# Turning the normalised x: VectorE's 32x32 blocks and DMAs in place of TensorE's transpose

## The chip, the core and the metric

One core of one Trainium2 chip. The core has TensorE (PE; its weight loads are listed as PEld), VectorE (DVE), ScalarE (ACT), GpSimd (POOL) and SyncE (SP), and 16 DMA engines. The metric is the device time of one execution in microseconds, lower is better; the time before is the median of 3 runs. A profile is one execution taken by the hardware profiler; its span runs from the first to the last instruction.

## What is computed

A cross-attention block followed by a feed-forward block, in float32, over 16 batches of 64 tokens with 512 features (1,024 tokens, handled as 8 tiles of 128).

```python
def layernorm(x): return (x - mean(x)) / sqrt(var(x) + 1e-5)

# attention: 32 heads of 128
q = layernorm(x) @ Wq;  k = ctx @ Wk;  v = ctx @ Wv          # 512 -> 4096 each
score = q k^T / sqrt(128) + position_bias;  masked softmax
x = x + (probs @ v) @ Wo                                     # 4096 -> 512
# feed-forward: a base layer and 8 low-rank experts with router weights
y = layernorm(x)
x = x + y @ base_W^T + base_b + experts(y)
```

The product `layernorm(x) @ Wq` needs the normalised x with its features on the partitions, so each tile [128 tokens, 512 features] must be turned. That turn is what the change touches.

## The kernel before, in words

**Matmuls.** Every large product is a float32 product split into a high and a low part (`split`, lines 69 to 71: ScalarE casts the high part, VectorE subtracts to get the low part), and each step is three TensorE matmuls (`mm3`, line 256). The K, V and Q projections also use a seven-product Strassen-Winograd scheme (`winograd`, line 213): seven steps in the order 1, 2, 6, 5, 7, 4, 3, with sums on VectorE or ScalarE after each (`post`): c11 after step 2, c22 after 7, c21 after 4, c12 after 3. c22 and c12 read the same PSUM bank `yb`: step 3 adds to it after c22 has been read.

**Stages.** First K and V for all heads, written to DRAM (`kd`, `vd`). The stages are listed in line 377: "k" stages (`keys_of`, 7 x 12 matmuls, weights `in_wk`) and "o" stages (values, 7 x 24 matmuls, weights `in_wv`). Each stage's weights are loaded two stages ahead, or as soon as buffers are free, and turned into sums (line 161 for wk, line 193 for wv) and hi/lo parts (`gh`, `gl`) one stage ahead. Results go out through 8 blocks of pool "ob" (kd stores at line 336, vd stores at 341). In the four key stages q = 3, 4, 5, 6 two tiles of x each are loaded (`x_tile`, line 321), normalised (`norm`, lines 87 to 100: statistics on VectorE, a power on GpSimd, the scaling on ScalarE) and turned (`x_turn`, line 325, called after steps 5 and 3). The stages q = 4 and q = 5 follow each other directly; q = 3 and q = 6 stand between value stages. The four 128x512 buffers of pool "v" hold x and its normalised copy, and later the loaded v.

**After it.** The turned x (`xT`) is read by GpSimd for eight differences (`tt`, line 132) and by ScalarE and VectorE for hi/lo parts, all for the query products, which begin beside the last key stage. Then, head pair by head pair, scores, softmax, the products with v and the output projection; in that part the probabilities are already turned by VectorE in 32x32 blocks, with four DMAs a head (`turned_p`, lines 490 to 502: `pb`, then `pt<-pb`). Last the feed-forward block.

**What sets the order.** TensorE's order is the program's (`manual_schedule`). In the K and V part the order on VectorE, ScalarE, GpSimd and on SyncE's queue, which issues all DMAs but one, is set when the program is built, by a scheduler with its own estimate of times; on the chip each engine and the queue run it strictly in that order. A DMA whose data isn't ready holds all that stand behind it in SyncE's queue. DMAs signal through eight completion semaphores used in turn.

Of the kernel before, what the change touches and what calls it, by code (L numbers as in the profile page):

```python
# [9 lines left out]
F32 = mybir.dt.float32  # L10
# [9 lines left out]
P = 128  # L20
D = 512
KC = D // P
# [25 lines left out]
def xattn_ffn_kernel(ctx: ExitStack, tc: tile.TileContext, x, ctxT, wq, wk, wv, wo, fside, mask,  # L48
                     base_wT, base_b, arT, router_b, lora_b, expert_map, out):
    nc = tc.nc  # L50
# [15 lines left out]
    def blk(tag, name, dt=F32, shape=(P, 512)):  # L66
        return pools[tag].tile(list(shape), dt, tag=tag, name=name)
# [34 lines left out]
    def transposed(ps, xn):  # L102
        for kc in range(KC):
            nc.tensor.transpose(ps[:, kc * P:(kc + 1) * P], xn[:, kc * P:(kc + 1) * P], ident)  # L104
# [4 lines left out]
    with ExitStack() as actx:  # L109
# [6 lines left out]
        def small_bank(name):  # L116
            return pss.tile([P, 512], F32, tag="s", name=name)
# [205 lines left out]
            return xn, xt  # L323

        def x_turn(t, xn):
            ps = small_bank("pst")
            transposed(ps, xn)
            a, g = divmod(t, 4)
            dst = xT.rearrange("p k (g a b) -> p g a k b", g=4, a=2)[:, g, a]
            nc.scalar.copy(dst, ps.rearrange("p (k b) -> p k b", k=KC))  # L330

        stored, copied = [], []

# [12 lines left out]
        with tc.manual_schedule(engines={nc.tensor.engine}):  # L346
# [15 lines left out]
            def keys_of(q, g):  # L362
                xn = {}
                for i in winograd(mm_weights(tc_, g), 2, emit_k(q)):
                    if 3 <= q < 7:
                        t = 2 * (q - 3)
                        if i in (1, 6):
                            xn[i] = x_tile(t + (i == 6))
                        if i in (6, 7):
                            with tc.issue_after(copied[-1].ins):  # L370
                                norm(sm, *([a] for a in xn[1 if i == 6 else 6]))
                        elif i == 5:
                            x_turn(t, xn[1][0])
                        elif i == 3:
                            x_turn(t + 1, xn[6][0])
# [61 lines left out]
            def load_v(p):  # L437
                v = []
                for w in range(4):
                    v.append(blk("v", "v", F32, (P, 2, 256)))  # L440
                    nc.sync.dma_start(out=v[w], in_=vd[p // 2][:, p % 2, 2 * w:2 * w + 2, :])
                return v
# [148 lines left out]
            v = load_v(0)  # L591
# [11 lines left out]
            for p in range(NP):  # L603
# [3 lines left out]
                for c in steps:  # L607
                    if c == "P":
# [3 lines left out]
                        v = load_v(p)  # L612
# [269 lines left out]
```

## Time and profile before

| | |
|---|---|
| median of 3 runs | 768.36 us (767.52 to 769.46) |
| the profiled execution: its time, its span | 768.93 us, 767.1 us |
| TensorE busy (share of the span) | 756.0 us (99%), granted clock 1.00 throughout |
| VectorE, ScalarE, GpSimd busy | 559.8 (73%), 416.8 (54%), 124.7 us (16%) |
| DMA | 80,849 packets, 124.68 MB, mean 163 GB/s |
| `pst<-ident,xn` on TensorE | 32 transposes of 128x128, 272 ns each, from 113 to 258 us |
| `xT<-pst` on ScalarE | 8 copies of 128x512, 586 ns each |
| `xn<-xt` on ScalarE | 8 of 128x512, 818 ns each |
| VectorE in 20 us stretches from 110 to 270 | 11.5 to 14.9 us busy |

How to read it: lines such as L336 are lines of the kernel. A group is line, engine, operation, out<-in and count; `ps<-wh,oh` means that tile ps is written from tiles wh and oh, with buffer numbers left out. SPq is SyncE's queue: its durations are those of issuing a DMA, while "to landing" is from the issue until the data has arrived. Matmuls overlap one another, so the durations of single matmuls add up to more than the time they take together. The chain of waits is followed back from the last instruction to whatever released each step.

### The profile page before, as it was taken

The numbers are of one execution on the slowest core, as the hardware profiler recorded it, in microseconds if no ns is written. First come the engines' busy times: TensorE is split into PE (matmuls) and PEld (weight loads), VectorE is DVE, ScalarE is ACT, GpSimd is POOL, SyncE is SP. The second block draws the span as 40 slices with busy tenths as digits, with TensorE's granted clock in tenths as the row PEclk, the third lists the DMA queues.
The fourth block names the chain that finished last, engine by engine and source line by source line (L and its number), as shares of the span: only waits on it lengthen the run. The fifth ranks groups of instructions, "written<-read, shape, count | busy, mean of one in ns | idle before, by whom it ended". The sixth has DMA issues, their size and how long they took to land.

```text
span 767.1 us, 16662 instructions
## 1 busy us (share of the span) xinstructions
PE 756.0 (99%) x6186; PEld 627.9 (82%) x6186; DVE 559.8 (73%) x1068; ACT 416.8 (54%) x1165; POOL 124.7 (16%) x143
## 2 busy tenths in 40 slices
PE   8999999999999999989999999999999999999998
PEld 6888888888888888867888888888887888888898
DVE  7986666566655765878778777787768777878975
ACT  6654455445554545667654665556545664475361
POOL 0000000000000522233220222022210222010330
PEclk9999999999999999999999999999999999999999
DMA  7785546464635446476544554446543654462011
GB/s 260 239 276 191 187 160 214 135 209 151 200 130 178 138 132 206 145 235 197 186 138 143 159 191 163 139 132 199 171 144 111 200 183 130 133 198 85 2 54 57
DMA packets 80849, 124.68 MB, mean 163 GB/s; under 512 B 9728, under 2 KB 30976, under 8 KB 80768
## 3 DMA queue, kind: packets, MB, share of 16 engines
q1 hardware_dynamic: 80624, 123.56, 49.7%
q8 instruction: 48, 0.79, 0.4%
q14 instruction: 33, 0.27, 0.1%
q10 hardware_dynamic: 144, 0.06, 0.0%
HBM read 83.74 MB, written 35.65 MB: 156 GB/s over the span
## 4 chain that ended last, share of the span: by engine, by line
PE 91%; DVE 4%; ACT 2%; issue 1%; DMA 1%; SPq 0%; POOL 0%; DVEq 0%; ACTq 0%; POOLq 0%
PE ps L259 73%; PE yz L259 5%; PE ps L728 5%; PE ps L513 4%; PE pss L466 4%; ACT p L477 1%; DMA cT<-in_ctxT 1%; PE pst L104 0%; DVE gl L71 0%; DVE bs L694 0%; DVE pb L494 0%; PE pt L104 0%; DVE p L485 0%; ACT bh L70 0%; DVE ol L71 0%
## 5 line engine op out<-in xcount | busy, mean ns | idle before, releaser
L530 DVE TENSOR_TENSOR acc<-acc,ps 128x512 f32<-128x512 f32 x128 | 87.0, 682 | 24.8 <-PE ps L259 24.0
L477 ACT ACTIVATE p<-p,nm 128x64 f32<-128x64 f32 x256 | 85.8, 338 | 34.0 <-DVE nm L471 31.7
L259 PE MATMUL ps<-wh,oh 128*128 128x512 f32 x256 | 100.1, 391 | 0.0
L259 PE MATMUL ps<-wh,ol 128*128 128x512 f32 x256 | 99.7, 390 | 0.1
L259 PE MATMUL ps<-wl,oh 128*128 128x512 f32 x256 | 99.7, 389 | 0.0
L70 ACT CAST gh<-s 128x512 fp32r<-128x512 f32 (+1 forms) x128 | 64.2, 514 | 62.7 <-PE ps L259 50.5
L71 DVE TENSOR_TENSOR gl<-s,gh 128x512 fp32r<-128x512 f32 (+1 forms) x128 | 70.5, 555 | 33.0 <-ACT gh L70 32.9
L161 POOL TENSOR_TENSOR s<-rq 128x256 f32<-128x256 f32 x32 | 25.2, 787 | 250.1 <-DMA rq<-in_wq 193.0
L71 DVE TENSOR_TENSOR ol<-ps,oh 128x512 fp32r<-128x512 f32 x64 | 39.8, 683 | 33.7 <-ACT oh L70 33.6
L71 DVE TENSOR_TENSOR gl<-raw,gh 128x512 fp32r<-128x512 f32 x48 | 34.6, 722 | 35.0 <-ACT gh L70 24.5
L70 ACT CAST gh<-raw 128x512 fp32r<-128x512 f32 x48 | 29.8, 622 | 53.9 <-PE yz L259 36.6
L259 PEld LDWEIGHTS ps<-wh,ol 128*128 128x128 f32 x256 | 48.1, 188 | 10.3 <-DVE ol L71 0.5
L259 PEld LDWEIGHTS ps<-wl,oh 128*128 128x128 f32 x256 | 48.1, 188 | 10.0
L259 PEld LDWEIGHTS ps<-wh,oh 128*128 128x128 f32 x256 | 48.0, 188 | 10.0
L477 ACT ACTIVATION_READ_ACCUMULATOR p<-p,nm 128x1 f32 x256 | 48.4, 189 | 0.0
L561 DVE TENSOR_TENSOR q<-u,ps 128x512 f32<-128x512 f32 x48 | 32.8, 684 | 21.2 <-PE ps L259 15.5
L457 POOL TENSOR_TENSOR bm<-bm,maskb 128x512 f32<-128x512 f32 x32 | 41.7, 1324 | 37.8 <-DMA bm<-in_fside 37.8
L96 POOL TENSOR_TENSOR rs<-rs,nhalf 128x1 f32<-128x1 f32 x8 | 4.4, 549 | 243.8 <-DVE rs L95 243.8
L70 ACT CAST gh<-rq 128x256 fp32r<-128x256 f32 x48 | 19.3, 404 | 37.3 <-PE ps L259 33.4
L70 ACT CAST oh<-ps 128x512 fp32r<-128x512 f32 x64 | 33.1, 589 | 11.3 <-PE ps L513 11.3
L513 PEld LDWEIGHTS ps<-pt,v 64*64 64x64 f32 x2048 | 32.1, 135 | 6.4 <-issue 6.4
L550 ACT COPY u<-ps 128x512 f32<-128x512 f32 x48 | 27.8, 579 | 17.1 <-PE ps L259 7.2
(259 smaller groups left out, 1989.3 us busy)
## 6 DMA issues: line engine op xcount, KB each, us to landing
kd<-c SPq DMA_DIRECT2D x64, 256.0 KB, 2.2
vd<-c SPq DMA_DIRECT2D x64, 256.0 KB, 2.6
kT<-kd SPq DMA_DIRECT2D x64, 256.0 KB, 4.1
v<-vd SPq DMA_DIRECT2D x64, 256.0 KB, 4.0
raw<-in_wk SPq DMA_DIRECT2D x32, 256.0 KB, 3.9
raw<-in_wv SPq DMA_DIRECT2D x32, 256.0 KB, 4.1
rq<-in_wq SPq DMA_DIRECT2D x32, 256.0 KB, 3.9
bm<-in_fside SPq DMA_DIRECT2D x32, 256.0 KB, 4.4
```

Source lines behind the costliest of these rows:

```text
L70: first = nc.scalar.copy(hi, src)
L71: return first, (lo_eng or nc.vector).tensor_tensor(lo, src, hi.bitcast(F32), ALU.subtract)
L161: self.eng.tensor_tensor(r, a, b, op)
L259: nc.tensor.matmul(o, lhsT=a, rhs=b, start=first and n == 0, stop=last and n == 2, skip_group_check=True)
L457: nc.gpsimd.tensor_tensor(bm, bm, maskb, ALU.add)
L466: nc.tensor.matmul(ps[a * S:(a + 1) * S, t, :], lhsT=qT[n // 8][:, cq], rhs=kT[m // 8][:, ck], start=True, stop=True)
L477: nc.scalar.activation(p[:, t, :], p[:, t, :], AF.Exp, bias=nm[:, t:t + 1], accum_out=sme[:, t:t + 1])
L513: nc.tensor.matmul(ps[a][d:d + S, t * S:(t + 1) * S], lhsT=v[t // 2][r, t % 2, c], rhs=pt[r, :, t, :], start=True, stop=True)
L530: return nc.vector.tensor_tensor(acc[:, t, :], acc[:, t, :], ps, ALU.add)
L550: copy = nc.scalar.copy(s[i], b["x"])
L561: add = nc.vector.tensor_tensor(self.blocks[key], s[u], b[bk], ALU.add)
L728: nc.tensor.matmul(o, lhsT=a, rhs=b, start=start, stop=stop, skip_group_check=True)
```

## The change

Only `x_turn` differs. Before, four TensorE transposes with the identity wrote a PSUM bank, and ScalarE copied the bank to its place in `xT`. Now VectorE transposes the tile in 32x32 blocks from `xn` into a new block `xb` (pool "v", the same four buffers), and 16 DMAs on SyncE's queue, one for each pair of block row i and block column j, carry 32 partitions x 4 runs of 32 floats to their place in `xT`.

```diff
         def x_turn(t, xn):
-            ps = small_bank("pst")
-            transposed(ps, xn)
+
             a, g = divmod(t, 4)
             dst = xT.rearrange("p k (g a b) -> p g a k b", g=4, a=2)[:, g, a]
-            nc.scalar.copy(dst, ps.rearrange("p (k b) -> p k b", k=KC))
+            xb = blk("v", "xb", F32, (P, 4, KC, 32))
+            nc.vector.transpose(xb, xn.rearrange("p (k j i) -> p j k i", k=KC, j=4))
+            for j in range(4):
+                for i in range(4):
+                    nc.sync.dma_start(out=dst[32 * j:32 * j + 32, :, 32 * i:32 * i + 32],
+                                      in_=xb[32 * i:32 * i + 32, j])
```

In the built program the scheduler's order around it moves too. On SyncE's queue the 16 DMAs of tiles 0, 1, 2, 3, 6 and 7 stand ahead of the stores of the steps that follow; those of tiles 4 and 5 stand together, 32 in a row, ahead of five wv loads (`raw<-in_wv`) that were issued earlier before. The loads of the later x tiles stand behind the DMAs of earlier ones. On VectorE the statistics of tile 2 stand ahead of a c22 sum, and a sum of two wv loads (line 193) stands between the first and the second c22 sum of the value stage that follows q = 5.

## The prediction

> **What bounds the kernel now.** I read the page's chain first, then the same chain in order of time around the change (90 to 320 us), then single lines and tiles, then the timelines of VectorE and of SyncE's queue. The chain:
>
> ```profile
> PE 91%; DVE 4%; ACT 2%; issue 1%; DMA 1%; SPq 0%; POOL 0%; DVEq 0%; ACTq 0%; POOLq 0%
> ```
>
> TensorE sets the end. In the stretch that the change touches it never pauses (20.00 us busy in every 20 us from 90 to 330), and its own transposes are links of the chain (start, length, what):
>
> ```profile
> 89.93 23.57 PE ps L259 x104
> 113.50 0.44 PE pst L104 x4
> 113.94 8.22 PE ps L259 x36
> 122.16 0.44 PE pst L104 x4
> ```
>
> So all that leaves TensorE here shortens the time, as long as nobody else then comes late. The question is who does; the change hands 128 DMAs to SyncE's queue, which issues in a fixed order, so I read what an issue costs there and on VectorE (min/median/max ns), and how long a landing takes:
>
> ```profile
> L336 SPq DMA_DIRECT2D kd<-c x64: 319/320/694, 17.6 to 324.2; - x64
> L341 SPq DMA_DIRECT2D vd<-c x64: 512/514/690, 56.8 to 297.6; - x64
> L501 SPq DMA_DIRECT2D pt<-pb x128: 507/584/1564, 338.0 to 705.2; - x128
> 344.32 2.41 SPq L501 DMA_DIRECT2D pt<-pb  x4
> L644 SPq DMA_DIRECT2D sar<-in_arT x2: 384/402/420, 668.8 to 669.2; - x2
> L494 DVE STREAM_TRANSPOSE pb<-p x32: 698/703/712, 336.6 to 701.9; 128x512 f32<-128x512 f32 x32
> raw<-in_wv SPq DMA_DIRECT2D x32, 256.0 KB, 4.1
> pt<-pb SPq DMA_DIRECT2D x128, 32.0 KB, 1.9
> ```
>
> pt<-pb is the nearest relative of the new DMAs: SBUF to SBUF, 32 partitions. Its issue is dearer (0.58) than a 128-row store to HBM (0.32). Four in a row took 2.41 us, 0.60 each with the gaps.
>
> **Removed from TensorE.** Eight groups of four 128x128 transposes. The chain gives a group 0.44 us; the period gives a little more: from the first transposes (113.34) to the next (122.00) are 8.66 us with 36 matmuls of 0.2267 between, which leaves 0.50. 8 x 0.50 = 4.0 us, all on the path. A rule speaks against the change here: the Trainium skill, "VectorE: DVE Perf Modes", The three transpose paths, gives TensorE 390 ns for one 128x128 bf16 transpose and VectorE 311 ns for blocks only, and advises TensorE for a full 128x128. By that figure 32 transposes would free 12.5 us; the trace's row, pipelined, frees 4.0. I take the row: the prize is 0.5%.
>
> ScalarE loses eight copies xT<-pst of 0.586 us; it was under 60% busy here, so that gives nothing. The bank of pss that a turn took isn't waited for either before or after.
>
> **Added on VectorE.** Eight block transposes of 0.70 us, 5.6 us in the 145 us from 113 to 258. In each 20 us there VectorE is busy 11.5 to 14.9; 0 to 1 us on the path, I take 0. If the cover were gone, it would be at most 5.6.
>
> **Added on SyncE: the step that decides.** Sixteen DMAs a tile. Their data is nothing: the trace's packet records have 11 ns for a 128-byte packet (five of them) beside 46 for 1 KB and 84 for 2 KB; 2,048 packets on 16 engines are an estimated 1.4 us a tile. The issue is what counts. Let d be the time from one of these issues to the next. From below 0.60, the pt<-pb row. For the third dimension (32x4x32, 128 runs of 128 bytes) the trace has two neighbours: sar<-in_arT, split in runs on one side, costs no more than a plain load (0.40 beside 0.33 to 0.42), but vd<-c costs 0.19 more than kd<-c. So d is 0.60 to 0.80; I take 0.64, since sar has the same kind of shape, and vd differs in rows (256) too. Sixteen are 10.2 us (at 0.80: 12.8), against 19.1 us for a whole key stage with two tiles, where SyncE has some 7 us of its own to issue.
>
> Here the Trainium skill, "DMA: Bandwidth & Descriptors", Anatomy of one DMA and Rules for kernel authors, also speaks against the change: about 2.0 us fixed per DMA, and below 64 KB mostly overhead. If one waited for another, 64 DMAs at 2.04 would be 131 us and the kernel would end far above 840. The row says that they overlap: 0.60 apart though each lands after 1.9. The built program has eight completion semaphores in turn, so each DMA waits for the one eight before it: 1.9/8 = 0.24 us, below d. I take the row.
>
> **Who stands behind them in the queue.** In the built program's order the first tile's 16 come before six kd stores, the second's before four vd stores, six wv loads, the next x tile and two wk loads. The stores have eight blocks, and a block is next wanted a stage later, so stores 10 us late hold nobody; the wk and wv loads run a stage or more ahead. At d = 0.64 that first burst has caught up by 147; VectorE's statistics of the third x tile, ahead of a c22 sum, wait perhaps a microsecond, with more than 5 to spare.
>
> The dangerous run is tiles 2 to 5, in two key stages that follow each other, 64 DMAs in one chain. Times are those of the trace, with TensorE ahead by 0.5 per turn removed:
> - Tile 2 normalised 170.5 - 1.0, block transpose 0.7: 170.4 with a little queueing. 16 x 0.64: 180.6. Six stores at 0.38: 182.9. 16 more: 193.1. Tile 4's load and two stores, 1.3; tile 5's load lands 2.9 later: 197.3.
> - VectorE is held at that tile's statistics. From there statistics, a weight sum, small steps, two c12 sums, one gl and the block transpose: 4.7 us, so tile 4 is turned at 202.0. The c12 sums are done by 201, wanted at 203.1.
> - 32 x 0.64 without a pause: 222.5. Behind them stand five wv loads; the fourth is issued 1.4 later and lands 4.1 after: 228.0.
> - In the new VectorE order the sum s of two of those loads stands in front of the c22 sum of the second block. Before:
>
> ```profile
> 223.72 0.69 DVE L193 TENSOR_TENSOR s<-raw,raw 128x512 f32<-128x512 f32 x1
> 225.91 0.69 DVE L232 TENSOR_TENSOR c<-u,ps 128x512 f32<-128x512 f32 x1 [0.72 <-ACT u L230]
> 234.57 0.39 PE L259 MATMUL ps<-gh,t3h 128*128 128x512 f32 x1
> ```
>
> That c22 must have read its bank before TensorE's step at 234.57, which is 231.6 after six turns are gone. It would be done at 228.0 + 0.7 + 0.7 = 229.4. So 2.2 us are left, and each 0.01 of d uses 0.64 of them: the cover is gone at d = 0.675, and behind it the stall is 64 x (d - 0.675).
>
> The last two tiles repeat the first burst. They are turned near 270 instead of 259; GpSimd's eight tt subtractions (12.2 us) then end near 284, and its next sum ran at 281.8 to 282.6 for a use on ScalarE after 299. Hidden. After 330 nothing differs but the start.
>
> **Sum.** -4.0 + 0 (VectorE) + 0 (queue, d = 0.64) = -4.0 on the profiled execution, 768.93 with a span of 767.1. The median of the runs is 768.36, 0.6 lower; on it the forecast is 764.4. I leave 0.2 for small waits: 764.6.
>
> **Rivals.**
> 1. *The queue of tiles 2 to 5 holds TensorE.* With vd's extra 0.19, d = 0.80: the chain ends 64 x 0.125 = 8.0 us late, -4.0 + 8.0 = +4.0, 772.4. It ends above before from d = 0.74 on. For it: pt<-pb is already dearer than any HBM issue, and vd shows that shape can cost 0.19. Against it: sar. With d = 0.85 it is 775.6, and I let the range end there.
> 2. *Partly eaten.* d between 0.70 and 0.775: the stall is 1.6 to 6.4, the time 766 to 771, middle 768.3.
> 3. *The gain is lost behind the stage.* TensorE is earlier by 4 at 330, but the first pair of heads has waits on ScalarE (3.1 us at 346) and on transfers; if one of those is fixed in time, half comes back: 766.5. Against it: all of them hang on chains that start from TensorE.
> 4. *VectorE becomes the bound* through the 5.6 us: it has over 5 us idle in each 20, so at most 770. Unlikely.
>
> **How the numbers follow.** Forecast, d up to 0.70: 0.46, 764.3 to 766. Rival 2: 0.17. Rival 1: 0.28. Rival 3: 0.05. Rival 4 and waits that I haven't seen: 0.04. A measurement of this kernel can tell about 0.3% (2.3 us) from no change, so the bounds are 766.1 and 770.7. Faster 0.46; same takes rival 3 and nearly all of rival 2, 0.19; slower takes rival 1, what is left of rival 2, and the unseen: 0.35. The likeliest case alone is 764.0 to 766.0; the range that should hold 8 in 10 is 763.9 to 775.6.
>
> **What would show it.** Right: no pst on TensorE's chain, 8 STREAM_TRANSPOSE of 0.70, xT<-xb issues 0.60 to 0.68 apart, TensorE without a gap from 90 to 330, and the wv loads behind the long burst issued near 222 to 224. Wrong: issues at 0.75 or more apart; TensorE waiting near 232 for a c22 sum, with VectorE idle on a wv load before it; or TensorE waiting near 203 for a c12 sum with VectorE idle on an x tile. A landing of these DMAs above 5 us would put the eight semaphores in charge, which my sum excludes.

## The result, and the profile after

The changed kernel takes 770.61 us (median of 8 runs, 768.48 to 771.78) against 768.33 for the kernel before beside it: ratio 1.0028, 95% interval 1.0016 to 1.0040. The profiled execution took 770.77 us with a span of 769.0; before it was 768.93 and 767.1. The forecast was 764.6. So the direction was wrong, and the text's first rival, the queue of tiles 2 to 5 that holds TensorE, is what came; but it came at an issue spacing at which the text had excluded it.

First the page's chain, shares of the span by engine:

```profile
PE 88%; DVE 4%; DMA 3%; SPq 2%; ACT 1%; issue 1%; POOL 0%; DVEq 0%; POOLq 0%; ACTq 0%
```

TensorE has given three points to transfers and SyncE's queue. The single lines (min/median/max ns, first and last start) show that the new parts cost what was forecast, and one thing besides:

```profile
L333 SPq DMA_DIRECT2D xT<-xb x128: 585/599/1712, 114.5 to 275.6; - x128
...
L330 DVE STREAM_TRANSPOSE xb<-xn x8: 702/703/715, 113.8 to 259.5; 128x512 f32<-128x512 f32 x8
...
L340 SPq DMA_DIRECT2D kd<-c x64: 319/327/2266, 17.9 to 326.2; - x64
```

Sixteen issues take 10.27 to 10.36 us, so d is 0.645; 0.64 was forecast. But the maxima of the first and third line, 1.71 and 2.27 us for one issue, both lie in the run of tiles 2 to 5. SyncE's queue there (start, length, what):

```profile
170.73 10.36 SPq L333 DMA_DIRECT2D xT<-xb  x16
181.19 3.01 SPq L340 DMA_DIRECT2D kd<-c  x6
184.26 10.27 SPq L333 DMA_DIRECT2D xT<-xb  x16
194.57 0.59 SPq L321 DMA_DIRECT2D xt<-in_x  x1
195.27 2.74 SPq L340 DMA_DIRECT2D kd<-c  x2
198.06 0.42 SPq L321 DMA_DIRECT2D xt<-in_x  x1
...
205.42 21.72 SPq L333 DMA_DIRECT2D xT<-xb  x32
227.19 2.49 SPq L188 DMA_DIRECT2D raw<-in_wv  x5
```

It is the order of the forecast, each piece a little later than there. VectorE behind it (in brackets, its idle time before the instruction and who ended that):

```profile
199.20 0.69 DVE L92 BATCH_NORM_STATS2 bs<-xt 128x6 f32<-128x512 f32 x1 [4.17 <-DMA xt<-in_x]
...
222.05 0.69 DVE L232 TENSOR_TENSOR c<-u,ps 128x512 f32<-128x512 f32 x1 [0.86 <-ACT u L230]
233.54 0.69 DVE L193 TENSOR_TENSOR s<-raw,raw 128x512 f32<-128x512 f32 x1 [10.81 <-DMA raw<-in_wv]
234.15 0.68 DVE L232 TENSOR_TENSOR c<-u,ps 128x512 f32<-128x512 f32 x1
...
248.07 1.27 DVE L223 TENSOR_TENSOR c<-u,ps 128x512 f32<-128x512 f32 x2
...
254.33 0.70 DVE L92 BATCH_NORM_STATS2 bs<-xt 128x6 f32<-128x512 f32 x1 [2.43 <-DMA xt<-in_x]
```

VectorE stands still for 10.81 us in front of a weight sum, with the c22 sum that TensorE needs right behind it. And TensorE:

```profile
234.89 0.50 PE L259 MATMUL ps<-gh,t3h 128*128 128x512 f32 x1 [2.62 <-DVE c L232]
...
257.82 0.50 PE L259 MATMUL ps<-t3h,gh 128*128 128x512 f32 x1 [0.65 <-DVE c L232]
```

The first wait is the c22 sum just seen; the second is one stage later, where the statistics of tile 7 stand before a c22 sum and wait 2.43 us for their x load. No burst stands right ahead of that load. It was issued at 249.75 behind two key stores whose sums VectorE, still late, made only at 248.07 (242.93 and 244.34 in the kernel before, where the load left at 245.48). Neither of TensorE's two waits exists in the kernel before. The busy time in stretches of 2 us (PE, PEld, DVE, ACT, POOL, then granted clock, DMA share, GB/s) shows a third loss:

```profile
232.00:234.00 2.00, 0.27 (x2) 0.00 (x0) 0.46 (x1) 0.00 (x0) 0.00 (x0) 1.00 0.97 355
...
236.00:238.00 2.00, 2.00 (x6) 1.63 (x5) 2.00 (x5) 1.95 (x5) 0.00 (x0) 0.50 1.16 355
```

Right after the wait TensorE is at half clock: six matmuls in 2 us, 0.43 apart where 0.227 is usual. The clock record says from 235.85 for 3.413 us. Half of that time, 1.7 us, is lost.

A ledger comes from the same bank copy of ScalarE (u<-ps) in both traces, after minus before:

| time in the kernel before | 111 | 147 | 189 | 216 to 225 | 240 | 265 to 327 | end of span |
|---|---|---|---|---|---|---|---|
| us | +0.3 | -0.7 | -1.6 | -2.5 | +2.1 | +2.0 | +1.9 |

Each pair of turns gives 0.9 to 1.0, as forecast. Between 225 and 240 it loses 4.6: the wait of 2.6, the half clock 1.7, and 0.3 that I put down to the refill of TensorE behind the wait. The pair of tiles 6 and 7 should have given 0.95 more and gave 0.1, because of the second wait.

### The profile page after: what moved, and what is told of

It reads as the page before. It is cut to its first block, busy times and chain, and to the rows that moved or that the text cites. A ratio compares the mean times of both kernels' runs of the same rounds, so it can differ in the third digit from the quotient of the medians.

```text
span 769.0 us, 16702 instructions
## 1 busy us (share of the span) xinstructions
PE 755.5 (98%) x6154; PEld 626.7 (81%) x6154; DVE 561.2 (73%) x1076; ACT 411.7 (54%) x1157; POOL 124.8 (16%) x143
## 4 chain that ended last, share of the span: by engine, by line
PE 88%; DVE 4%; DMA 3%; SPq 2%; ACT 1%; issue 1%; POOL 0%; DVEq 0%; POOLq 0%; ACTq 0%
PE ps L259 70%; PE yz L259 5%; PE ps L732 5%; PE ps L517 4%; PE pss L470 4%; SPq L333 1%; DVE gl L71 1%; ACT p L481 1%; DMA cT<-in_ctxT 1%; DMA slb<-in_lora_b 1%; DMA raw<-in_wv 1%; DMA xt<-in_x 1%; DVE bs L698 0%; PE pt L104 0%; DVE s L161 0%
## 5 line engine op out<-in xcount | busy, mean ns | idle before, releaser
L71 DVE TENSOR_TENSOR gl<-s,gh 128x512 fp32r<-128x512 f32 (+1 forms) x128 | 72.1, 567 | 24.5 <-ACT gh L70 24.3
```

The costliest lines, as they stand in the source:

```text
L71: return first, (lo_eng or nc.vector).tensor_tensor(lo, src, hi.bitcast(F32), ALU.subtract)
```

## The experiments

Ten kernels, in three groups that each shared a chip with the kernel before (768.75, 769.12 and 769.26 us). The queue theory ("theory A" in four of the texts): what stands behind the issues in SyncE's queue lands late, VectorE, which works in a fixed order, waits for it, and TensorE then waits for VectorE. The rival, the order theory (B): the added work of VectorE and the rearranged order cost by themselves. The scheduler set the order anew for each of these kernels, so none of them holds the order of VectorE fixed.

**one_dma**: the sixteen become one, which leaves out the exchange of the blocks between partitions.

```diff
-            for j in range(4):
-                for i in range(4):
-                    nc.sync.dma_start(out=dst[32 * j:32 * j + 32, :, 32 * i:32 * i + 32],
-                                      in_=xb[32 * i:32 * i + 32, j])
+            nc.sync.dma_start(out=dst, in_=xb.rearrange("p j k i -> p (j k i)").rearrange("p (k b) -> p k b", k=KC))
```

> One DMA a tile in place of 16; VectorE's block transposes stay, and so does the removal of TensorE's. Leaves out the exchange of blocks between partitions. Theory A (the 16 issues a tile on SyncE's queue make the wv loads and x loads late, and TensorE then waits for c22 sums): nothing is late, 764.6 +- 0.8, no TensorE wait for a c22 sum, clock 1.00 until 340. Theory B (the added VectorE work or the reordered engines cost the time, not the queue): 769 to 771.

Measured: 764.82 us, ratio 0.9952 (0.9934 to 0.9971). VectorE's block transposes are all there, and the forecast's 764.6 is met; so the transposes cost nothing that shows. The order did change: the weight sum of 233.54 stands ahead of both c22 sums here (also in eight, five and pool_queue), as in the kernel before. That place is no kinder to a late load, so it does not explain the gain; no run here shows more of the order by itself. VectorE's waits for transfers (total us, times, longest), first in the changed kernel:

```profile
DVE bs L92 <- DMA xt<-in_x: 14.9, 6, 5.4
DVE s L193 <- DMA raw<-in_wv: 13.2, 3, 10.8
```

and with one DMA:

```profile
DVE s L193 <- DMA raw<-in_wv: 2.1, 2, 1.3
...
DVE bs L92 <- DMA xt<-in_x: 1.3, 1, 1.3
```

The lateness of x and wv loads is gone with the issues.

**eight** and **twenty** change the number of issues. eight: two DMAs for each 32 partitions, not exchanged. twenty: the four diagonal blocks are cut in two.

```diff
+            for c in range(4):
+                for h in range(2):
+                    r = slice(32 * c, 32 * c + 32)
+                    nc.sync.dma_start(out=dst[r, 2 * h:2 * h + 2, :], in_=...)
```

> Eight DMAs a tile in place of sixteen, each of twice the bytes; it leaves out the exchange of blocks between partition groups, so the same bytes go to other places. Queue theory: a tile takes 5.1 us of SyncE's queue, a pair 10.3; the chain that ended 2.6 us late with 41 us of issues for four tiles is 20 us shorter, so no load is late: 764.8 us, 763.8 to 766.5, as with one and with five. If the loss grows in proportion to the issues (0 at 1, 5.8 at 16), 767.5. Order theory: 768 to 771.

```diff
+                for i, ks in ((i, ks) for i in range(4) for ks in (((0, 2), (2, 4)) if i == j else ((0, 4),))):
+                    ks = slice(*ks)
+                    nc.sync.dma_start(out=dst[32 * j:32 * j + 32, ks, 32 * i:32 * i + 32],
+                                      in_=xb[32 * i:32 * i + 32, j, ks])
```

> Twenty DMAs a tile: each diagonal block goes in two halves, same bytes. Theory A: the chain of tiles 2 to 5 is 16 x 0.645 = 10.3 us longer, with no cover left: 780 to 783, TensorE's wait near 235 grows from 2.6 to about 13. Theory B: 770.5 to 771.5, since neither VectorE nor the bytes change.

Measured: eight 765.44, ratio 0.9951 (0.9921 to 0.9982); twenty 777.71, ratio 1.0124 (1.0104 to 1.0144). The loss is no slope but a cover that runs out: nothing at 1 and at 8, then 2.3 us above before at 16 and 9.0 at 20 (1.4 at 12, the next run). With eight, VectorE does wait for x loads, and yet TensorE never pauses between 90 and 330 us:

```profile
DVE bs L92 <- DMA xt<-in_x: 12.5, 3, 6.8
```

The time of twenty is under the 780 to 783 of its text, which also had the wrong wait: VectorE waits 15.90 us for a wv load, but the c22 sums stand ahead of it there, and the late one is another again. SyncE's queue:

```profile
221.69 13.75 SPq L334 DMA_DIRECT2D xT<-xb  x20
235.49 3.43 SPq L188 DMA_DIRECT2D raw<-in_wv  x7
239.02 10.61 SPq L346 DMA_DIRECT2D vd<-c  x14
```

ScalarE wants a free block for its c21 copy, and that block is freed by a vd store of the last row:

```profile
244.81 1.94 ACT L236 COPY c<-ps 128x512 f32<-128x512 f32 x3 [13.13 <-DMA vd<-c]
```

TensorE waits 8.8 us for that copy, where the text had some 13 us on a c22 sum. The prediction let late stores hold nobody; with twenty issues a tile they do.

**diag12**: GpSimd copies the four diagonal blocks, which need no exchange; twelve DMAs are left.

```diff
+            for j in range(4):
+                r = slice(32 * j, 32 * j + 32)
+                nc.gpsimd.tensor_copy(dst[r, :, r], xb[r, j])
+                for i in range(4):
+                    if i != j:
+                        nc.sync.dma_start(out=dst[r, :, 32 * i:32 * i + 32], in_=xb[32 * i:32 * i + 32, j])
```

> Twelve DMAs a tile: the four blocks on the diagonal need no change of partition and are copied by GpSimd, idle in this stretch. The chain of tiles 2 to 5 is 16 issues of 0.645 shorter, 10.3 us, where the wait that TensorE saw was about 3. Theory A: 764.4 to 766. Theory B: 769 to 771, and GpSimd's copies on top change nothing.

Measured: 770.15, ratio 1.0017 (1.0007 to 1.0028). Missed: a quarter fewer issues gained nothing that is clear of the intervals. No TensorE wait for a c22 sum is left, but a new one of 3.0 us on ScalarE:

```profile
195.15 0.81 ACT L100 ACTIVATE xn<-xt,nb,rs 128x512 f32<-128x512 f32 x1 [2.58 <-DVE nb L98]
195.87 0.56 ACT L230 COPY u<-ps 128x512 f32<-128x512 f32 x1
```

The x load of tile 4 was behind 24 issues, statistics and xn came late, and ScalarE has a bank copy (u) behind xn.

**loads_first** gives the wv loads that held VectorE a place ahead of the last burst.

```diff
-                load(n + 2)
+                with tc.high_priority(offset=600 if n == 6 else 0):
+                    load(n + 2)
```

> All 16 DMAs a tile stay; only the wv loads of the last value stage get a higher priority, so that they stand ahead of the 32 DMAs of tiles 4 and 5 in SyncE's queue. Theory A with the order as cause: the wait near 235 goes, 2.6 + 1.7 of slow clock with it; the second wait (0.65, for the statistics of tile 7) may stay: 765 to 767. If it's the mere number of issues, wherever they stand: 770 to 772.

Measured: 770.74, ratio 1.0039 (1.0025 to 1.0052). Missed. wv no longer holds anybody; x does instead (24.8 us in all, 14.9 in the changed kernel):

```profile
DVE bs L92 <- DMA xt<-in_x: 24.8, 6, 10.5
...
PE ps L259 <- DVE c L232: 4.0, 1, 4.0
```

and TensorE waits 4.0 us for a c22 sum behind those statistics. So my first form of the queue theory, "the wv loads behind the long burst", fell. What is left is the general one: the queue is full there, and here mending one transfer's place made another late.

**spread**: all sixteen, but four at a time behind the key and value stores.

```diff
+        def some(store, n=4):
+            with tc.issue_after(store.ins):
+                for o, i in pend[:n]:
+                    nc.sync.dma_start(out=o, in_=i)
+            del pend[:n]
+            return store
...
-                stored[:] = [nc.sync.dma_start(out=kd[4 * q + 2 * i + k][:, j * HALF:(j + 1) * HALF], in_=c)]
+                stored[:] = [some(nc.sync.dma_start(out=kd[4 * q + 2 * i + k][:, j * HALF:(j + 1) * HALF], in_=c))]
```

> The same sixteen DMAs a tile on the same queue, but let out four at a time behind the key and value stores that follow the turn, not in one burst. If the length of the burst is what makes the next load late (10.4 us for one, 21.7 us for the two that follow each other), no load stands behind more than 2.4 us of them at a time and nothing is late: 764.6, 763.8 to 767. If the sum of the issues before a load is what counts, spreading them changes nothing for a load that stands behind all of them: 768.5 to 772 as after, with a wait of some microseconds of TensorE on a c22 or c12 sum of VectorE.

Measured: 771.35, ratio 1.0038 (1.0023 to 1.0053). The time fits the second reading: not the length of one burst, but the sum of the issues ahead of a load. Tile 2's sixteen issues, in four groups from 175.71 on, still stand ahead of the load of tile 4. It was issued at 189.14 (181.37 in the kernel before), VectorE's statistics waited 3.69 us for it, and TensorE 2.13 us for the bank copy behind that tile's xn.

**queue_only**: the kernel before, its turn kept, and sixteen DMAs of xn a tile into an unused DRAM tensor. It tests the queue without anything on VectorE.

```diff
             nc.scalar.copy(dst, ps.rearrange("p (k b) -> p k b", k=KC))
+            xs, src = (s.rearrange("p (k j i) -> p j k i", k=KC, j=4) for s in (scr[t], xn))
+            for j in range(4):
+                for i in range(4):
+                    nc.sync.dma_start(out=xs[32 * i:32 * i + 32, j], in_=src[32 * i:32 * i + 32, j])
+
+        scr = [dram.tile([P, 512], F32, tag=f"scr{t}", name=f"scr{t}") for t in range(NT)]
```

> The kernel before, its turn by TensorE and ScalarE kept, and sixteen more DMAs a tile on SyncE's queue at the same place (pieces of the normalised tile, 32 partitions each, stored to an unused DRAM tensor); VectorE has nothing new. Queue theory: after the change TensorE gained 4.0 us and yet the kernel lost 2.3 by the medians, so the queue alone is worth +6.3: 774.6 us, 772 to 777, with VectorE waiting over 10 us for x and wv loads and TensorE for a c22 or c12 sum. If stores to DRAM are issued nearer 0.5 us (as the key stores are), a burst takes 8 us in place of 10.3 and little is late: 769 to 772. Order theory (VectorE's transposes and what they displace are what costs): 768.4, as before.

Measured: 779.39, ratio 1.013 (1.010 to 1.016), dearer than either reading. The chain in order of time:

```profile
194.30 0.59 SPq L321
...
195.46 4.20 DMA kd<-c
199.65 0.81 ACT xn L100
...
200.50 1.12 PE pst L104 x4
```

The x load of tile 4 leaves at 194.30, behind two bursts; its landing lets VectorE go on at 197.62 and ScalarE make xn at 199.64 (the view puts this stretch down to a store). TensorE's transposes stand in TensorE's own order and wait 8.83 us for xn. Half clock from 195.85 for 10.24 us comes with it. That wait does not exist in the changed kernel. So this run is no pure price of the queue in the changed kernel: with its turn gone from TensorE's order, the same lateness reaches TensorE only by VectorE's sums and ScalarE's copies.

**pool_queue** and **act_queue** issue the same sixteen from GpSimd and from ScalarE.

```diff
-                    nc.sync.dma_start(out=dst[32 * j:32 * j + 32, :, 32 * i:32 * i + 32],
+                    nc.gpsimd.dma_start(out=dst[32 * j:32 * j + 32, :, 32 * i:32 * i + 32],
```

> The sixteen DMAs of a tile are issued by GpSimd, SyncE's queue holds what it held in the kernel before. Queue theory: no x, wv or store transfer is late any more, so 764.6, 763.8 to 767, if GpSimd issues at up to about 1.2 us each (19 us a tile against 24 us between tiles): only the 0.6 us power of the next tile's statistics stands behind them on GpSimd. At 1.5 us or more each the tiles pile up, the power comes late, the normalised tile and with it VectorE come late: 770 to 790. The DMA page of the skill is not needed for either end: the issue cost on GpSimd is what this run measures. Order theory: 768 to 771 whatever the queue.

> The sixteen DMAs of a tile are issued by ScalarE, among its casts and bank copies, up to eleven in a row. At 0.6 us each that is 9.6 us a tile for an engine that is busy 9.2 of 20 us in this stage; a bank copy or a cast that stands behind eleven issues is 6.6 us late, more than the 2 to 3 us that TensorE is ahead of its banks, so each tile costs 2 to 5 us: 780 to 805. If an issue on ScalarE costs 0.1 us or less, nothing is late: 764.6 to 766.

Measured: pool_queue 766.8, ratio 0.9974 (0.9962 to 0.9986); act_queue 808.25, ratio 1.0505 (1.0485 to 1.0525). On GpSimd an issue is busy 0.548 us and sixteen take 8.69. SyncE is as before, and the kernel is faster than before, not by the whole 4 us: the power for the next tile stands behind a burst (182.56 to 191.25), and ScalarE waits with xn and a bank copy behind it:

```profile
192.11 0.82 ACT L100 ACTIVATE xn<-xt,nb,rs 128x512 f32<-128x512 f32 x1 [4.00 <-issue]
...
193.34 0.58 ACT L230 COPY u<-ps 128x512 f32<-128x512 f32 x1
```

TensorE waits 1.33 us for that copy. This run also answers a rival that the texts of the runs leave out, that the traffic of the 128-byte pieces makes the other loads land late: the pieces are the same, and VectorE waits 3.1 us for x loads and 0.9 for wv (14.9 and 13.2 in the changed kernel). On ScalarE an issue takes 0.61 us (median), and TensorE waits four times, 8 to 9 us each:

```profile
PE ps L259 <- ACT u L230: 34.9, 4, 9.4
```

Each of them also brings 10.24 us at half clock, partly after the wait, which my 780 to 805 did not have.

**five**: the exchange goes through DRAM. One store of the turned tile, then four loads, each 32 partitions with rows of 512 bytes; xT is laid out by blocks of 32 tokens, and the first stage of the queries reads it so.

```diff
+            nc.sync.dma_start(out=xd[t], in_=xb.rearrange("p j k b -> p (j k b)"))
+            turn_rest()
+            pend.append((t, 4 * (2 * g + a)))
...
+        def turn_rest():
+            for t, n in pend:
+                for j in range(4):
+                    nc.sync.dma_start(out=xT[32 * j:32 * j + 32, n:n + 4],
+                                      in_=xd[t].rearrange("(i p) (j f) -> j p i f", i=4, j=4)[j])
+            pend.clear()
```

> The turn in five DMAs a tile in place of sixteen: VectorE's turned tile is stored to DRAM as it stands, and four loads bring it back exchanged, one for each 32 partitions (xT is laid out by blocks of 32 tokens for that, and the first stage of the queries reads it in runs of 32). Queue theory (what holds TensorE is the number of issues that stand in SyncE's queue before the x, wv and store transfers): 40 issues a run in place of 128; a pair of tiles takes 10 x 0.6 = 6 us of the queue in place of 20.6, so 14 us come off the chain that ended 2.6 us late, and nothing waits for c22: 764.6 us, 763.8 to 766, as with one DMA a tile. If SyncE waits at each reload for its store to land, at most 2.5 us a tile are added, 5 a pair, still 9 us less than sixteen: the same time. Order theory (the rearranged work of VectorE is what costs): 768 to 771, as with sixteen.

Measured: 765.2, ratio 0.9935 (0.9910 to 0.9960), 3.9 us below before: the fastest of the kernels that make the whole turn. From 90 to 330 us TensorE never pauses:

```profile
90.00:330.00 240.00, 240.00 (x1115) 198.65 (x1114) 162.08 (x272) 119.15 (x219) 29.08 (x26) 1.00 0.55 188
```

(236.74 in the changed kernel.) The reload of a tile is put off to the next turn, so no issue waits for the store: a load's issue is 0.45 us (median), 1.8 us for four.

## Why the prediction failed

*Right.* The removal: 0.9 to 1.0 us per pair of turns. VectorE's transposes: 0 (one_dma, eight, five). The spacing d: 0.645 for 0.64, and the eight semaphores don't bind (landing 1.8 us, median). The chain of tiles 2 to 5, with the place of the stall and the two instructions in it, and the sign named as "wrong", TensorE waiting near 232 for a c22 sum: that wait began at 232.27.

*The step that failed: "So 2.2 us are left ... the cover is gone at d = 0.675".* The c22 sum ended at 234.83, not 229.4. Term by term, both ends of each:

| term | forecast | measured | late by |
|---|---|---|---|
| first burst begins | 170.4 | 170.73 | 0.3 |
| first burst, stores, second burst end | 193.1 | 194.53 | 1.1 more |
| to the statistics of tile 5 | 4.2 | 6.81 | 2.6 |
| to tile 4 turned | 4.7 | 4.1 | -0.6 |
| 32 issues | 20.5 | 21.72 | 1.2 |
| to the fourth wv load landed | 5.5 | 6.4 | 0.9 |

Together 5.4 us, against a cover of 2.2 (2.9 as it came out: TensorE arrived at 232.27, not 231.6); the rest is the wait of 2.62. d has 0.3 of it. The larger parts are single long issues (2.27 in the third row, 1.71 in the fifth), stores at 0.50 each behind a burst where 0.38 was taken, and landings a little slower. The prediction's own row for pt<-pb showed a maximum of 1.56 us beside the median of 0.58; with 64 new and some 20 old issues in one chain, I summed medians. I also tied the fate of the cover to d alone, so the rival got its chance from vd's shape and its price from d = 0.80, where queueing and landing could do the same at 0.645.

*Not counted at all: what follows a wait.* Stall to gain was set at one to one; the wait of 2.62 cost 4.6. And the text took the last two tiles for a repeat of the first burst: tile 7's x load was late too, since VectorE had not caught up, and a wait of 0.65 us took most of that pair's 0.95.

*The rival's size.* At 772.4 it was 1.8 too high, with a stall of 8.0 in place of two waits of 3.3 together and a slow clock. That the wide range holds the result is luck in part: the rival that opened it needed d = 0.74 or more, which did not come.

What stays open: why one issue in some dozens takes 1.2 to 2.3 us; they occur in all kernels here, on loads, stores and turns, in the kernel before only from 347 us on. After 346 the traces drift against each other by about 1 us both ways. The 1.2 us that the changed kernel loses near 348 come with a second slow period (last section). Of the 1.1 that it wins back near 577, 0.87 is a pause of TensorE in the kernel before in which it waited for nothing that the profile shows; its reason is open.

## What to carry to other kernels

A fixed-order queue is a resource with a sum: before many small DMAs go on it, add up the issues that stand ahead of every load and store with a consumer in a fixed order, at the mean with its long tail and not at the median, and ask for the cover of each. When that sum is over the cover, moving one transfer forward, spreading the burst or taking away too few issues only changed who was late (loads_first, spread, diag12); far fewer issues (five, eight) or a queue with less behind it (pool_queue) mended it. And a wait of TensorE can be dearer than its length.

## What the runs showed of the hardware

The half clock. In the clock records of these profiles every slow period, but for those cut off by the end, lasts 3.413 us or two or three times that (6.827, 10.240), and the time between two is a whole multiple too (109.226 = 32 x 3.4133, 191.146 = 56 x 3.4133). So it is decided on a grid of 3.413 us. Where that grid lies differs from profile to profile. Laid on it, TensorE's waits sort themselves by the idle time within one window, not by their length:

| kernel, wait ended at | wait | in one window | slow after it |
|---|---|---|---|
| after, 234.89 | 2.62 | 2.45 | yes |
| after, 348.53 | 3.09 | 3.05 | yes |
| spread, 195.73 | 2.13 | 2.13 | yes |
| one_dma, 342.46 | 2.57 | 1.99 | yes |
| diag12, 346.58 | 1.98 | 1.93 | yes |
| five, 17.91 and 19.06 | 1.21 and 0.66 | 1.87 | yes |
| before, 346.53 | 3.11 | 1.94 and 1.17 | no |
| pool_queue, 343.93 | 2.02 | 1.75 | no |
| pool_queue, 193.97 | 1.33 | 1.33 | no |

The edge lies near 1.9 us idle in a window of 3.41, and no sharper than 0.1 (1.87 slow, 1.94 not); the other waits over 0.9 us from 10 us on fall on the same sides of it. Once the clock is slow, less keeps it so: after a window with 0.97 us idle (loads_first, from 256.78) it stayed slow for one more. The kernel before has the longest of these waits and pays nothing, since two windows share it. The changed kernel has the same wait, in one window, and pays. Before:

```profile
346.53 0.50 PE L259 MATMUL ps<-t6h,gh 128*128 128x512 f32 x1 [3.11 <-ACT u L550]
```

After:

```profile
348.53 0.79 PE L259 MATMUL ps<-t6h,gh 128*128 128x512 f32 x1 [3.09 <-ACT u L554]
```

So this second period comes of where the grid lay; the first stands behind a wait that only the changed kernel has. All eight runs of the changed kernel have a mean granted clock of 0.993 to 0.995, and 74 of the 76 runs of the kernel before beside the experiments have 0.997 to 1.000. A slow period takes an estimated 0.002 of the mean (half of 3.413 us in a span of 769), so these are about two or three periods against one or none. The Trainium skill, "TensorE: Matmul & The Clock Gate", What's actually happening, has the same window, free-running, 3413 ns, with half rate after an idle one; the length agrees. By the rule under HAM oscillation on the same page, no idle gap above some 3.4 us, none of the waits in the table would cost anything. Here 1.93 us in one window brought a slow period (diag12), and the one behind 2.45 us cost 1.7 us more, so the measurement decides.
